# Layer 0's last two periods with output tiles between matrices, layer 1's group norm per image, first pixels loaded into room given up early

## The chip, the cores and the metric

The kernel runs on one core of one Trainium2 chip. The metric is device time in microseconds (us), the median of several runs. A core has five engines that work side by side: TensorE (PE, matrix products; its weight loads are listed apart as PEld), VectorE (DVE), ScalarE (ACT), GpSimd (POOL) and SyncE (SP), which here only issues DMA transfers. Tiles live in SBUF, products land in PSUM.

## The reference

Two images x of 512 channels and 64 x 64 pixels pass two layers, each of the form x = x + f(gn(x)); gn is a group norm of 32 groups without weights.

Layer 0's f is a deformable convolution:

```
xproj  = gn(x) @ in_w + in_b
x1     = gelu(layernorm(depthwise3x3(gn(x)) + dw_b))
offset = x1 @ off_w + off_b
mask   = softmax over 9 points of (x1 @ mask_w + mask_b), in 16 groups
out    = sum over 9 points of mask * bilinear sample of xproj at (grid + offset)
result = out @ out_w + out_b
```

Layer 1's f is attention over the 4096 pixels of an image, then a batch norm and a relu:

```
q, k = tanh(px @ Wq.T), tanh(px @ Wk.T)          # 64 wide
v    = px @ Wv.T
attn = softmax(einsum(q, k, align_w))
c    = (px + attn @ v) @ Wfc.T + bfc
f    = relu(gamma * (c - mean) * rsqrt(var + eps) + beta)
```

The change leaves the computation as it is.

## The kernel before, in words

**Layer 0** handles an image in 8 chunks of 512 pixels (8 rows), 16 chunks for both images. The stages of one chunk are Python generators, which give their instructions step by step:

- `project(i)`: the group-normed rows `xn`, and their products with `in_w` (PSUM `pq`), stored to DRAM as `xt_d`.
- `features(i)`: depthwise convolution on DVE from `xn`, layer norm, gelu.
- `weights(i)`, 27 steps: four products `po` with their additions to `o` (steps 1 to 8), the softmax's exponential (9), `tx` (10), an overflow sum called far here (11), the softmax's sums (12), `my` (13), nine steps that build the 5 x 5 weight windows `aw` out of `pk` (14 to 22), the copy `at` on ACT (23), and four transposes `p_tr` with copies to `awT` (24 to 27).
- `sample(i)`, 24 steps: eight small products `pb`, each copied into the matrix `bt` (1 to 8; all copies on ACT, but for the last chunk every second on DVE); eight products `pa` of `bt` with a fetched patch, each with four copies to `dT` (9 to 16); and the four **output tiles** `py`, the products with `out_w`, each followed by an addition to the residual `res`, its statistics into `stats2`, and the store to `x1_d` (17 to 24). The fetch of the next chunk's patches and the reads of `res` are issued inside these steps, on SP.

In layer 0's main loop the order is written out by hand (`tc.manual_schedule()`). `period(...)` takes steps of `sample(i)` (m), `weights(i + 1)` (w), `features(i + 2)` and `(i + 3)`, `project(i + 3)`, the last four transposes of `weights(i)` (v) and the output tiles of `sample(i - 1)` (y). From i = 13 on there is nothing left to project, and in i = 14 and 15 there are no features left: the period's calls for them give nothing, but the order of the rest stays. In period 14, m is chunk 14, w chunk 15, y chunk 13; in period 15 m is chunk 15, w is empty and y chunk 14. The output tiles of chunk 15 come after the loop, in `y.rest()`. Every engine is given its instructions in the order written.

**Between the layers.** Layer 0's pools are closed and layer 1's opened in the same memory. By default the first use of a pool's room waits for all tiles of closed pools that the pool lies over; with `reuse_waits="tile"` a tile waits only for those that it lies over itself. Layer 1's pixel pool `w1c` has 8 places of 8 KB, at the lowest addresses after the constants, where layer 0 keeps `xn`, `bt`, `awT` and small weights. The code then issues, on SP: the loads of `wkq` (the key and query weights side by side, in both orders) and `al`; the first two chunks of pixels (L1140); `wc`, the joined value and output weights (L1158); the next two chunks. DVE gathers both images' statistics (L1182), and `group_norm` with PE, DVE and ACT turns them into scale and shift (L602 to L620). Then ACT normalizes the first two chunks (L1173), DVE forms their sums and differences (L1151 to L1154) and those of `wc` (`wcs`, L1165 to L1168); these serve a seven-product scheme for 2 x 2 block matrices.

**Layer 1** per image: four turns of key and query products `pk` (L1305) and four `values` calls each, of seven products `pv` (L1251) in PSUM banks A0 to A5 with sums on DVE; then eight query blocks of scores (`pS`, L1211), exponentials and products `acc` (L1364) and `p` (L1402); last the batch norm over both images.

Of the kernel before, what the change touches and what calls it, by code (L numbers as in the profile page):

```python
# [9 lines left out]
F32 = mybir.dt.float32  # L10
# [7 lines left out]
P = 128  # L18
NB = 2
C = 512  # L20
KB = C // P
# [10 lines left out]
NCH = S // CH  # L32
# [5 lines left out]
DQ = 64  # L38
# [486 lines left out]
NSEQ = NB * NCH  # L525
# [45 lines left out]
def window_path(ctx: ExitStack, tc: tile.TileContext, t_in: dict, out: bass.AP, far: bass.AP, sums: bass.AP):  # L571
    nc = tc.nc
# [23 lines left out]
    nc.vector.memset(eps, EPS)  # L596
    stats2 = [const.tile([P, KB, NCH, 6], F32, name=f"stats2_{n}") for n in range(NB)]

    def group_norm_steps(mv, k, small, psum, result):
# [30 lines left out]
    with ExitStack() as l0:  # L630
# [8 lines left out]
        xt_d = [dram.tile([WIN, WIN, C], F32, name=f"xt_{n}") for n in range(NB)]  # L639
        xn = wp.tile([P, KB, ROWS + 2, W], F32, name="xn")  # L640
        bt = wp.tile([P, G, 2 * PX, PR * PC], F32, name="bt")

# [10 lines left out]
        in_w = load_w("L0_conv_in_w", C, wp)  # L653
        in_b = load("L0_conv_in_b", [P, KB], t_in["L0_conv_in_b"].rearrange("(kb p) -> p kb", p=P), wp)
# [343 lines left out]
        def period(y, v, m, w, f, g, p, more):  # L998
# [52 lines left out]
            w()  # L1051

        def value_weights():

# [46 lines left out]
    with ExitStack() as l1, tc.manual_schedule():  # L1101
        cp = l1.enter_context(tc.tile_pool(name="w1c", bufs=NCH))
        bnp = l1.enter_context(tc.tile_pool(name="w1bnp", bufs=1))
# [6 lines left out]
        with ExitStack() as at, ExitStack() as inner:  # L1110
            aw = at.enter_context(tc.tile_pool(name="w1w", bufs=1))
            wk = at.enter_context(tc.tile_pool(name="w1work", bufs=2))
            iw = inner.enter_context(tc.tile_pool(name="w1in", bufs=1, side="right"))
            vw = inner.enter_context(tc.tile_pool(name="w1v", bufs=3, side="right"))
# [6 lines left out]
            class Bank:  # L1121


                def tile(self, shape, dtype, tag, name):
                    return ps.tile(shape, dtype, tag="A1", name=name)
# [12 lines left out]
            def chunk(n, ch):  # L1138
                t = cp.tile([P, KB, CH], F32, tag="c", name="xt")
                (nc.scalar if n else nc.sync).dma_start(t, x1_d[n][ch])  # L1140
# [35 lines left out]

            pixels = {0: load_pixels(0, 0)}
# [110 lines left out]
            for n in range(NB):  # L1288
# [9 lines left out]
                for i in range(NCH // 2):  # L1298
# [4 lines left out]
                    for h in range(2):  # L1303
                        for kb in range(KB):
                            nc.tensor.matmul(  # L1305
                                pk[:, h, :], wkq[:, h, kb].rearrange("p h d -> p (h d)"), pixels[i][0][h][:, kb, :],
                                start=(kb == 0), stop=(kb == KB - 1),
                            )
# [224 lines left out]
```

## Time and profile before

| what | us |
|---|---|
| median of 3 runs | 3701.71 (3700.44 to 3704.26) |
| the profiled execution | 3707.44 |
| its span | 3705.6 |
| PE busy | 3417.9 (92%) |
| DVE busy | 2345.8 (63%) |
| ACT busy | 1304.1 (35%) |
| start of period 14's first output product (`py` L969) | 1150.55 |
| end of layer 0's last `py` | 1276.0 |
| first `pv` of layer 1 | 1293.31 |

Times in the trace count from the span's start. A line of the page's part 2 shows the span in 40 slices of 92.6 us. In a timeline a row is one run of like instructions: start, length, engine, line, what is written and read, how many; in brackets how long the engine was idle before and what released it. In a table of stretches a row gives the busy time of each engine, the granted TensorE clock (1.00 is full speed), and the share of the DMA engines. One `pb` or `pa` or `py` shows as several instructions: 16 in a row are a pair of `pb`, 16 are one `pa`, 8 are one `py` or one `po`.

### The profile page before, as it was taken

The numbers are of one execution on the slowest core, as the hardware profiler recorded it, in microseconds if no ns is written. First come the engines' busy times: TensorE is split into PE (matmuls) and PEld (weight loads), VectorE is DVE, ScalarE is ACT, GpSimd is POOL, SyncE is SP. The second block draws the span as 40 slices with busy tenths as digits, with TensorE's granted clock in tenths as the row PEclk, the third lists the DMA queues.
The fourth block names the chain that finished last, engine by engine and source line by source line (L and its number), as shares of the span: only waits on it lengthen the run. The fifth ranks groups of instructions, "written<-read, shape, count | busy, mean of one in ns | idle before, by whom it ended". The sixth has DMA issues, their size and how long they took to land.

```text
span 3705.6 us, 39010 instructions
## 1 busy us (share of the span) xinstructions
PE 3417.9 (92%) x15151; PEld 2433.8 (66%) x15151; DVE 2345.8 (63%) x3575; ACT 1304.1 (35%) x1691; POOL 291.0 (8%) x190
## 2 busy tenths in 40 slices
PE   4689998999998799999999999999999999999990
PEld 1355555555555477777777777777777777777770
DVE  5798989999996475545554554567455455545544
ACT  2476777787886321111111111221111111111114
POOL 2112111212111030000000000022000000000000
PEclk9789999999999899999999999999999999999995
DMA  7233442342432444334334333444433333243349
GB/s 240 63 98 114 135 137 83 115 133 83 127 109 78 142 157 171 126 129 139 123 108 163 122 125 130 140 155 169 149 121 111 122 138 111 101 149 121 111 162 389
DMA packets 180181, 500.06 MB, mean 135 GB/s; under 512 B 22640, under 2 KB 64368, under 8 KB 170512
## 3 DMA queue, kind: packets, MB, share of 16 engines
q1 hardware_dynamic: 176496, 473.34, 37.5%
q10 hardware_dynamic: 3456, 24.12, 1.7%
q8 instruction: 121, 1.98, 0.2%
q14 instruction: 76, 0.62, 0.0%
q0 software_dynamic: 32, 0.00, 0.0%
HBM read 406.09 MB, written 91.29 MB: 134 GB/s over the span
## 4 chain that ended last, share of the span: by engine, by line
PE 75%; DVE 15%; DMA 4%; ACT 2%; SPq 1%; issue 1%; POOL 1%; ACTq 0%; DVEq 0%; POOLq 0%
PE acc L1364 41%; DVE conv L788 8%; PE pS L1211 7%; PE p L1402 7%; PE py L969 5%; PE pq L758 4%; PE pa L949 4%; PE pv L1251 3%; PE pk L1305 1%; PE p_mean L801 1%; DVE pk L885 1%; DVE aw L890 1%; DMA patch<-xt 1%; DMA out<-ct 1%; DVE o L847 1%
## 5 line engine op out<-in xcount | busy, mean ns | idle before, releaser
L1364 PE MATMUL acc<-e,v 128*128 128x256 f32 x3072 | 768.2, 386 | 0.0
L1215 ACT ACTIVATE e<-pS 128x1024 f32<-128x1024 f32 x256 | 262.0, 1024 | 1386.4 <-PE pS L1211 1313.0
L1364 PE MATMUL acc<-tt,v 128*128 128x256 f32 x3072 | 748.2, 380 | 0.5 <-DMA v<-wv 0.5
L1364 PEld LDWEIGHTS acc<-e,v 128*128 128x128 f32 x3072 | 566.5, 190 | 233.2 <-issue 165.3
L1364 PEld LDWEIGHTS acc<-tt,v 128*128 128x128 f32 x3072 | 582.4, 190 | 91.2 <-issue 10.6
L1218 DVE TENSOR_TENSOR t<-e 128x256 f32<-128x256 f32 x256 | 108.8, 425 | 761.1 <-ACT e L1215 761.1
L788 DVE SCALAR_TENSOR_TENSOR conv<-xn,L_conv_dw_w_sb,conv 128x504 f32<-128x504 f32 (+1 forms) x512 | 399.7, 795 | 48.5 <-ACT conv L783 36.5
L1228 DVE TENSOR_TENSOR tot<-tot,e 128x512 f32<-128x512 f32 x480 | 330.1, 688 | 8.3
L949 PEld LDWEIGHTS pa<-bt,patch 96*128 96x128 f32 x2048 | 251.8, 197 | 63.1 <-issue 39.4
L1211 PE MATMUL pS<-q,kq 64*128 64x512 f32 x1024 | 289.0, 641 | 0.0
L949 PE MATMUL pa<-bt,patch 96*128 96x128 f32 x2048 | 255.3, 281 | 9.3 <-ACT dT L960 5.8
L935 ACT COPY bt<-pb 96x1024 f32<-96x1024 f32 x124 | 234.2, 2001 | 58.9 <-PE pb L930 58.9
L758 PE MATMUL pq<-L_conv_in_w_sb,xn 128*128 128x512 f32 x512 | 236.3, 605 | 4.3 <-ACT xn L748 4.3
L969 PE MATMUL py<-dT,L_conv_out_w_sb 128*128 128x512 f32 x512 | 238.0, 610 | 0.0
L1402 PE MATMUL p<-t,v 128*128 128x256 f32 x1024 | 231.4, 382 | 1.7 <-DMA v<-wv 1.7
L1402 PEld LDWEIGHTS p<-t,v 128*128 128x128 f32 x1024 | 192.1, 190 | 48.5 <-issue 21.2
L960 ACT COPY dT<-pa 32x256 f32<-32x256 f32 x496 | 179.5, 362 | 89.8 <-PE pa L949 80.9
L842 PE MATMUL po<-om_w_pg,feat 128*128 128x432 f32 x512 | 203.4, 542 | 0.0
L969 PEld LDWEIGHTS py<-dT,L_conv_out_w_sb 128*128 128x128 f32 x512 | 99.3, 197 | 119.6 <-issue 115.5
L758 PEld LDWEIGHTS pq<-L_conv_in_w_sb,xn 128*128 128x128 f32 x512 | 94.1, 194 | 109.5 <-issue 93.0
L842 PEld LDWEIGHTS po<-om_w_pg,feat 128*128 128x128 f32 x512 | 93.0, 191 | 90.5 <-issue 89.4
L1211 PEld LDWEIGHTS pS<-q,kq 64*128 64x128 f32 x1024 | 77.1, 184 | 84.9 <-issue 84.9
(203 smaller groups left out, 3731.2 us busy)
## 6 DMA issues: line engine op xcount, KB each, us to landing
v<-wv SPq DMA_DIRECT2D x252, 768.0 KB
patch<-xt SPq DMA_DIRECT2D x256, 192.0 KB
v<-wv SPq DMA_DIRECT2D x256, 128.0 KB
wv<-v SPq DMA_DIRECT2D x32, 896.0 KB
xt<-xj SPq DMA_DIRECT2D x128, 128.0 KB
res<-in_x SPq DMA_DIRECT2D x64, 256.0 KB
wx<-res SPq DMA_DIRECT2D x64, 256.0 KB
xq<-wx SPq DMA_DIRECT2D x16, 1024.0 KB
```

The lines of the kernel that those rows point to most:

```text
L758: nc.tensor.matmul(pq, xn[:, kb, 1 + 2 * t : 3 + 2 * t, :].rearrange("p r c -> p (r c)"), in_w[:, kb, :], start=(kb == 0), stop=(kb == KB ...
L788: nc.vector.scalar_tensor_tensor(dst, src, wt, dst, ALU.mult, ALU.add)
L842: nc.tensor.matmul(po[:, : 3 * GP], f[:, kb, t * P : (t + 1) * P], om_w[:, kb].rearrange("p a k g -> p (a k g)"), start=(kb == 0), stop=(k ...
L935: copy(bt[:SN].rearrange("s g q d -> s d (g q)")[:, d0 : d0 + 4, :], pb[:SN])
L949: nc.tensor.matmul(pa[:, p], xp[:SN, p, cb * P : (cb + 1) * P], bt[:SN, 4 * cb : 4 * cb + 4, PX * s + p, :], start=True, stop=True,)
L960: copy(dst, src)
L969: nc.tensor.matmul(py, out_w[:, kb, cb * P : (cb + 1) * P], dT[:, kb, :], start=(kb == 0), stop=(kb == KB - 1))
L1211: nc.tensor.matmul(pS[:, h, :], kq[r, 2 * (kp // 4) + h, c0 : c0 + P], qs[qb][r, :], start=True, stop=True)
L1215: nc.scalar.activation(e.rearrange("p a q -> p (a q)"), pS.rearrange("p h q -> p (h q)"), AF.Exp)
L1228: nc.vector.tensor_add(tots[qb], tots[qb], e2[:, h, :])
L1364: nc.tensor.matmul(acc[j][:, cb * HQ : (cb + 1) * HQ], v[:, j, cb * P : (cb + 1) * P], ops[j], start=(kp + cb == 0), stop=(kp + cb == NPAI ...
L1402: nc.tensor.matmul(p7[:, cb * HQ : (cb + 1) * HQ], v7[:, cb * P : (cb + 1) * P], t3, start=(k + cb == 0), stop=(k + cb == NPAIR + 2),)
```

## The change

Four parts, in the order in which they run:

- `wkq` and `al` move from layer 1's pool `w1in` to the constants. `wkq` holds three matrices (key, query, key) instead of four, and a slice of two of them gives either order. They are loaded by SP ahead of layer 0's main loop, in five transfers instead of six.
- `in_w` gets its room right after `xn`, ahead of `bt`; its load stays where it was.
- Periods 14 and 15 get functions of their own. `next_to_last` takes chunk 15's eight `po` steps ahead of chunk 14's transposes, and chunk 13's output tiles between the pairs of `pb`. `last_period` takes chunk 14's output tiles between the pairs of chunk 15's `pb`, and between these steps those of a group norm of image 0, whose statistics are complete after period 8.
- At the border, `w1c` and `w1in` take `reuse_waits="tile"`; the first two chunks of pixels are loaded from ACT's queue instead of SP's; image 0's norm is there already, and image 1's is spread over four places of image 0's `values` calls, with a product in bank A5.

```diff
+    norm0 = []
+    wkq = const.tile([P, KB, 3, DQ], F32, name="wkq")
+    al = const.tile([P, 1], F32, name="al2")
...
         xn = wp.tile([P, KB, ROWS + 2, W], F32, name="xn")
+        in_w = wp.tile([P, KB, C], F32, name="in_w")
         bt = wp.tile([P, G, 2 * PX, PR * PC], F32, name="bt")
...
+        def next_to_last(y, v, m, w):
+            y()
+            w(8)
+            v(4)
+            for steps, tiles in ((1, 2), (1, 2), (2, 2), (1, 1)):
+                m(2)
+                w(steps)
+                y(tiles)
+            for _ in range(4):
+                m(2)
+                w(2)
+            w(2)
+
+        def image_norm(n):
+            mv = const.tile([P, KB, 2], F32, name=f"mv2_{n}")
+            for k in range(KB):
+                nc.vector.bn_aggr(mv[:, k, :], stats2[n][:, k, :, :].rearrange("p a b -> p (a b)"))
+            yield
+            yield from group_norm_steps(mv, KB, const, ps, norm0)
+
+        def last_period(y, v, m, _):
+            norm = image_norm(0)
+            y()
+            v(4)
+            for steps in (2, 2, 2, 1):
+                m(2)
+                y(steps)
+                next(norm, None)
+            for _ in range(8):
+                m()
+                next(norm, None)
+            for _ in norm:
+                pass
...
         fetch(0, 1)
+        for k, name in enumerate(("wkT", "wqT", "wkT")):
+            nc.sync.dma_start(wkq[:, :, k, :], t_in[name].rearrange("(kb p) m -> p kb m", p=P))
+        for h in range(2):
+            nc.sync.dma_start(al[h * DQ : (h + 1) * DQ, :], t_in["L1_conv_align_w"])
...
+                if i + 2 >= NSEQ:
+                    (next_to_last if i + 1 < NSEQ else last_period)(y, v, m, w)
+                    y, v = m, w
+                    continue
                 period(y, v, m, w, f, g, Chain(project, i + 3), lambda: next(later, None))
...
-        cp = l1.enter_context(tc.tile_pool(name="w1c", bufs=NCH))
+        cp = l1.enter_context(tc.tile_pool(name="w1c", bufs=NCH, reuse_waits="tile"))
...
-            iw = inner.enter_context(tc.tile_pool(name="w1in", bufs=1, side="right"))
+            iw = inner.enter_context(tc.tile_pool(name="w1in", bufs=1, side="right", reuse_waits="tile"))
...
-            wkq = iw.tile([P, 2, KB, 2, DQ], F32, name="wkq")
-            al = iw.tile([P, 1], F32, name="al2")
-            for h in range(2):
-                nc.sync.dma_start(wkq[:, h, :, h, :], t_in["wkT"].rearrange("(kb p) m -> p kb m", p=P))
-                nc.sync.dma_start(wkq[:, h, :, 1 - h, :], t_in["wqT"].rearrange("(kb p) m -> p kb m", p=P))
-                nc.sync.dma_start(al[h * DQ : (h + 1) * DQ, :], t_in["L1_conv_align_w"])
...
-                pair = [chunk(n, 2 * i + h) for h in range(2)]
+                pair = [chunk(n, 2 * i + h, nc.scalar if n or i == 0 else nc.sync) for h in range(2)]
...
-            mv = bnp.tile([P, NB * KB, 2], F32, name="mv2")
-            for k in range(NB * KB):
-                nc.vector.bn_aggr(mv[:, k, :], stats2[k // KB][:, k % KB, :, :].rearrange("p a b -> p (a b)"))
-            both = group_norm(mv, NB * KB, bnp, Bank())
-            norms = [[t[:, n * KB : (n + 1) * KB] for t in both] for n in range(NB)]
+            def second_norm():
+                mv = bnp.tile([P, KB, 2], F32, name="mv2")
+                for k in range(KB):
+                    nc.vector.bn_aggr(mv[:, k, :], stats2[1][:, k, :, :].rearrange("p a b -> p (a b)"))
+                yield
+                yield from group_norm_steps(mv, KB, bnp, Bank(), norms[1])
+            norms = [norm0, []]
+            later = second_norm()
...
                         values(n, i, t)
+                        for _ in range({5: 1, 7: 2, 11: 2, 12: 1}.get(4 * i + t, 0) if n == 0 else 0):
+                            next(later, None)
```

More of the change, by code (lines that the diff above doesn't have):

```diff
@@ L652, in window_path @@
                 eng.dma_start(img[kb][:, h * (S // 2) : (h + 1) * (S // 2)], x_v[0, :, kb, h * (S // 2) : (h + 1) * (S // 2)])
-        in_w = load_w("L0_conv_in_w", C, wp)
+        nc.sync.dma_start(in_w, t_in["L0_conv_in_w"].rearrange("(kb p) m -> p kb m", p=P))
         in_b = load("L0_conv_in_b", [P, KB], t_in["L0_conv_in_b"].rearrange("(kb p) -> p kb", p=P), wp)
@@ L1124, in tile, with chunk @@
                 def tile(self, shape, dtype, tag, name):
-                    return ps.tile(shape, dtype, tag="A1", name=name)
-            wkq = iw.tile([P, 2, KB, 2, DQ], F32, name="wkq")
-            al = iw.tile([P, 1], F32, name="al2")
-            for h in range(2):
-                nc.sync.dma_start(wkq[:, h, :, h, :], t_in["wkT"].rearrange("(kb p) m -> p kb m", p=P))
-                nc.sync.dma_start(wkq[:, h, :, 1 - h, :], t_in["wqT"].rearrange("(kb p) m -> p kb m", p=P))
-                nc.sync.dma_start(al[h * DQ : (h + 1) * DQ, :], t_in["L1_conv_align_w"])
+                    return ps.tile(shape, dtype, tag="A5", name=name)
+            pixels = {}
             ones = iw.tile([P, P], F32, name="ones_k")
             nc.vector.memset(ones, 1.0)
-            def chunk(n, ch):
+            def chunk(n, ch, queue):
                 t = cp.tile([P, KB, CH], F32, tag="c", name="xt")
-                (nc.scalar if n else nc.sync).dma_start(t, x1_d[n][ch])
+                queue.dma_start(t, x1_d[n][ch])
                 return t
             def load_pixels(n, i):
-                pair = [chunk(n, 2 * i + h) for h in range(2)]
+                pair = [chunk(n, 2 * i + h, nc.scalar if n or i == 0 else nc.sync) for h in range(2)]
                 return pair, [cp.tile([P, 2, 2, CH], F32, tag="c", name=name) for name in ("xsa", "xsb")]
@@ L1175, in normalize @@
                     )
-            pixels = {0: load_pixels(0, 0)}
+            pixels[0] = load_pixels(0, 0)
             wc = value_output()
             pixels[1] = load_pixels(0, 1)
-            mv = bnp.tile([P, NB * KB, 2], F32, name="mv2")
-            for k in range(NB * KB):
-                nc.vector.bn_aggr(mv[:, k, :], stats2[k // KB][:, k % KB, :, :].rearrange("p a b -> p (a b)"))
-            both = group_norm(mv, NB * KB, bnp, Bank())
-            norms = [[t[:, n * KB : (n + 1) * KB] for t in both] for n in range(NB)]
+            def second_norm():
[6 more added lines that the diff above has]
+            later = second_norm()
             w7 = aw.tile([P, 2, 7, HC], F32, name="w7")
@@ L1305, in window_path @@
                             nc.tensor.matmul(
-                                pk[:, h, :], wkq[:, h, kb].rearrange("p h d -> p (h d)"), pixels[i][0][h][:, kb, :],
+                                pk[:, h, :], wkq[:, kb, h : h + 2].rearrange("p h d -> p (h d)"), pixels[i][0][h][:, kb, :],
                                 start=(kb == 0), stop=(kb == KB - 1),
```

## The prediction

> **What bounds the kernel now.** I read the page's slices first. TensorE is busy nearly throughout, but for the prologue, the end, and a dip where layer 0 gives way to layer 1 (slices 13 and 14, 1111 to 1297 us); the same slices granted less clock.
>
> ```profile
> PE   4689998999998799999999999999999999999990
> PEclk9789999999999899999999999999999999999995
> ```
>
> The table of stretches then shows what the dip is made of:
>
> ```profile
> 1140.00:1150.00 10.00, 4.20 (x25) 4.01 (x24) 9.65 (x13) 8.30 (x11) 0.00 (x0) 0.73 0.57 184
> ...
> 1154.60:1165.00 10.40, 7.40 (x37) 4.58 (x37) 1.45 (x2) 7.34 (x7) 1.43 (x1) 0.68 0.38 140
> 1165.00:1180.00 15.00, 14.93 (x77) 7.41 (x75) 1.85 (x4) 11.38 (x7) 0.00 (x0) 1.00 0.00 1
> 1213.00:1240.00 27.00, 17.80 (x107) 13.82 (x108) 8.46 (x7) 11.31 (x11) 0.00 (x0) 0.50 0.24 72
> ...
> 240.00:250.00 10.00, 8.07 (x46) 4.54 (x45) 8.30 (x13) 8.03 (x9) 1.44 (x1) 1.00 0.73 236
> 1276.00:1293.30 17.30, 9.31 (x20) 4.39 (x21) 8.02 (x20) 7.33 (x10) 0.00 (x0) 0.80 0.91 334
> ```
>
> The first number after the length is PE's busy time, the eighth column the clock. From 1213 to 1240 no engine is busy for more than two thirds: PE waits, and what it does runs at half clock. TensorE's timeline gives the waits and two prices of each product:
>
> ```profile
> 1096.42 1.14 PE L930 MATMUL pb<-awT,sel 25*96 25x256 f32 x16 [0.83 <-ACT awT L902]
> ...
> 1150.55 4.07 PE L969 MATMUL py<-dT,L_conv_out_w_sb 128*128 128x512 f32 x8
> 1156.94 2.42 PE L901 MATMUL p_tr<-ident,at 128*128 128x128 f32 x16 [2.33 <-ACT at L893]
> ...
> 1213.85 3.67 PE L901 MATMUL p_tr<-ident,at 128*128 128x128 f32 x16 [4.92 <-ACT at L893]
> 1218.20 2.05 PE L930 MATMUL pb<-awT,sel 25*96 25x256 f32 x16 [0.68 <-ACT awT L902]
> 1222.18 2.12 PE L930 MATMUL pb<-awT,sel 25*96 25x256 f32 x16 [1.93 <-ACT bt L935]
> ...
> 1234.29 6.64 PE L949 MATMUL pa<-bt,patch 96*128 96x128 f32 x32 [2.01 <-ACT bt L935]
> ```
>
> A pair of `pb` costs 1.06 to 1.14 at full clock, 2.05 here; two `pa` 6.64 against 3.58. At the border:
>
> ```profile
> 1284.74 8.73 PE L1305 MATMUL pk<-xt,wkq 128*128 128x512 f32 x16 [3.78 <-ACT xt L1173]
> 1293.31 1.89 PE L1251 MATMUL pv<-wc,xt 128*128 128x256 f32 x8
> 1295.74 1.99 PE L1251 MATMUL pv<-wcs,xsa 128*128 128x256 f32 x8 [0.55 <-DVE wcs L1166]
> ```
>
> Layer 0's last `py` ends at 1276.0; `pk` starts 8.7 us later, at part clock. Here SP's queue decides: the pixel loads stand behind the last stores of `res` (issued from 1277.24, first used at 1283.83, 6.6 us for two), while the group norm runs beside them and ends at 1283.3. Behind 1316 PE never stands still for long, and layer 1's code per block is untouched: what counts is when the `pv` begin.
>
> [...] 1.00 drops to 0.50 behind the idle 1140.8 to 1147 and 1208.8 to 1213.8, stays there at some 50% busy, and returns after about 5 us of solid work; the stretch from 240 shows 1.00 kept at 81% busy. [...]
>
> **The change, part by part.** Every duration is the trace's, full clock unless said.
>
> *Period 14, from 1150.55.* The period's start doesn't move, since period 13 is untouched. Chunk 13's first `py` ends at 1154.6; the clock is back at about 1152. Now four `po` follow at once, 4 x 3.10 = 12.4, to 1167.0 (their gelu ended at 1149.5), where PE waited 2.33 and then ran cold. Chunk 14's transposes (1.97) and the last `awT` copy (0.8) come behind them, to 1169.8: 9.9 later than before. From there ACT sets the pace: eight `bt` copies of 1.86 (14.9), the exponential with its table load (1.96), the far sum (1.35), the first pair 1.1 and handshakes 0.8 give 1189.9, against 1180.5. PE has in this stage 4 x 1.06 + 3 x 3.44 = 14.6, so three `py` are hidden that before stood between the `pa`. Eight `pa` of 1.79 then end at 1204.4 (before: 1205.3). DVE: its last addition ends near 1186, then 0.77 + 8 x 1.57 = 13.3 of windows to 1199.3, hidden. ACT's `at` copy stands behind the last `dT` copies (1206.0) and takes 2.92: 1208.9, against 1213.8. Of 12.4 moved into idle time, 4.9 remain. PE's first `py` of chunk 14 fits ahead of it.
>
> *Period 15.* Transposes and copies: first `pb` at 1212.5 (before 1218.2, cold). Three rounds of a pair and a `py`, 4.5 each, plus 0.36 for the norm's first product: 1226.4; the copies, 1.86 on ACT and DVE side by side, hide under the `py`. Fourth pair and its copies, 1.06 + 2.1: 1229.5. Eight `pa` 14.3; the norm's root on ACT puts 1.6 (table load 1.28, 0.3) between their copies, and these alternate between ACT and DVE, so add 1.6 and 1.4: 1246.8. Four `py` 13.75, with up to 1.6 for the last `dT` copies: 1262.0 against 1276.0. **Gain so far 14.0**; of it 8.5 is clock (transposes 1.7, four pairs 4 x 1.0, `pa` 3.0), which I take as given because no gap on this path exceeds 2 us.
>
> The norm's aggregation and small DVE steps (1.0, 0.9) and second product (0.39) lie under `py`, `bt` copies and the wait for the last `bt`; uncovered they would add 2.3. SP: fetching chunk 15's patches (5.6 us per half) starts when a patch is free, about 1197 and 1204, and is needed at 1229 and 1239; the `res` reads move with their steps and keep some 8 us. What is late next is ACT's `bt` copies in period 14.
>
> *Border.* Places 0 and 1 of the pixel pool (16 KB) lie within `xn` and `in_w` (18 KB), read last at about 1118 (convolution) and 1092 (`pq`). ACT is through with its `dT` copies at 1248.4, issues two loads, which land 6.6 later at 1255, and normalizes eight times 0.72 to 1261: all under the last `py`. Nothing else waits on ACT there. The PSUM pool keeps its default wait, so `pk` needs the last addition of `res` (0.2 + 0.75): 1263.0, then 16 x 0.43 = 6.9 to 1269.9. SP's next issue is `wc`; before it went out 4.27 after the last `py`, held by the landing of `res`, so now at 1266.3, and takes 5.2 (the second image's: 2439.96 to 2445.16): 1271.5. There the `pv` begin, with 1.6 idle. DVE's four sums (4.7) are over by 1268.5; two `wcs` (1.4) by 1272.9, and the third product comes at 1273.2, before 1295.74. **Gain 22.5.**
>
> *Given back.* Image 1's norm inside the `values` calls: two small products 0.75 on PE, two table loads (2.6) on ACT, whose calls leave it some 3 of 6 us idle; 1.0. ACT meets `wfcT` earlier: the loads behind `wc` are 4 MB at about 400 GB/s (the border's DMA rate), landing near 1278.5, up to 5 us after ACT wants them; six PSUM banks take most, 1.0. The early loads of `wkq`: some 3 us of SP issue ahead of period 0, where SP already stands idle (109 to 114) or waits 26 us for a place; bounds -1 to +3, I take 0.5.
>
> Sum: 22.5 - 1.0 - 1.0 - 0.5 = 20.0. Span 3705.6 - 20.0 = 3685.6; the profiled execution reports 3707.44 and the median is 3701.71, so I set **3681.7** against the median.
>
> **Rivals.**
> *The early room is not there (transfer as late as before).* If the pixel tiles still wait for the end of layer 0, or the ACT queue reaches them late, they land 6.8 after the last `py`, the sums follow the normalizing, and the third product is again 19.7 behind it: 8.5 lost, 3690.2. For it: the loads were issued only at 1277.24. Against: they stood behind stores on SP, and the overlapped tiles are long dead.
> *ScalarE becomes the bound.* Period 14 is paced by ACT with 18.2 us of copies and sums; if handshakes or `pa` behind it cost as much as the reorder saves, in both periods, the 14.0 goes and the border's 8.5 less 2.5 stays: 3695.7. For it: 9.9 us of delay to `awT`. Against: period 15 shares its copies with DVE.
> *TensorE stays at half clock (slower).* In the new periods PE works about 91 us at full clock from 1154.6 to the end (`po` 12.4, transposes 4, `pb` 8.5, 7 + 4 `py` 38, `pa` 28.6). The ACT-paced stage leaves it 75 to 80% busy. Each us of that work done at half rate costs one more; from 20 us of it on the gain is gone, from 27.4 it is slower by over 0.2%; with a third of it, 30 us, 3711.7. For it: before, 17.8 busy us of 27 stayed at 0.50. Against: 81% kept 1.00.
>
> **How the numbers follow.** The likeliest course 0.68, its own range 3677 to 3687 (clock and handshakes +-3, `wc` +-2). Late pixels 0.14 at 3690. ScalarE 0.09 at 3696, which is within 0.2% (7.4 us, about what a measurement of this kernel can tell from no change: 3694.3 to 3709.1). Half clock 0.07 at 3712. A smaller rest (0.02) lies lower. Faster 0.84, same 0.09, slower 0.07. The range takes in the first two: 3674 to 3693.
>
> **What would show it.** In the profile after: four `po` in a row behind the `py` at 1150.6; `bt` copies on ACT without a break to about 1190; clock 1.00 from 1155 to the border; `py` between the pairs of `pb`; last `py` ending near 1262; two loads on ACT's queue near 1248, `pk` about 1 us behind the last `py`, `pv` 8 to 10 behind it. Wrong if the pixel loads are issued after the last `py`, if `at` of chunk 15 ends after 1212, if the clock reads 0.50 in period 15, or if `pv` in image 0 stand waiting for banks by more than 3 us.

## The result, and the profile after

The changed kernel takes **3686.89 us** (median of 5 runs, 3683.94 to 3688.61) against 3701.71 before: 14.8 us less, a ratio of 0.9958 with a 95% interval of 0.9947 to 0.9969. In a second series it was 3689.50 against 3703.27, 0.9961 [0.9947, 0.9975]. The two profiled executions lie further apart, 3685.08 against 3707.44 (spans 3683.3 and 3705.6); the experiments say why, as far as it is known.

The slices of the page of the kernel after, TensorE's busy share and its clock:

```profile
PE   4589998999998999999999999999999999999990
PEclk9789999999999999999999999999999999999995
```

The dip at slices 13 and 14 is gone from both lines. TensorE's timeline of the kernel after, from period 14 to the first values products (start, length, what, and in brackets the idle time before it):

```profile
1149.52 4.06 PE L976 MATMUL py<-dT,L_conv_out_w_sb 128*128 128x512 f32 x8
1153.42 11.76 PE L849 MATMUL po<-om_w_pg,feat 128*128 128x432 f32 x32
1165.02 1.96 PE L908 MATMUL p_tr<-ident,at 128*128 128x128 f32 x16
...
1187.88 17.99 PE L956 MATMUL pa<-bt,patch 96*128 96x128 f32 x128 [3.78 <-ACT bt L942]
1205.70 3.60 PE L976 MATMUL py<-dT,L_conv_out_w_sb 128*128 128x512 f32 x8
1210.37 1.99 PE L908 MATMUL p_tr<-ident,at 128*128 128x128 f32 x16 [1.07 <-ACT at L900]
...
1230.58 17.07 PE L956 MATMUL pa<-bt,patch 96*128 96x128 f32 x128 [1.76 <-ACT bt L942]
...
1262.28 7.10 PE L1356 MATMUL pk<-xt,wkq 128*128 128x512 f32 x16 [0.89 <-issue]
1270.09 1.97 PE L1302 MATMUL pv<-wc,xt 128*128 128x256 f32 x8 [0.70 <-DMA wc<-wvfc]
...
1294.42 1.13 PE L1302 MATMUL pv<-wc,xsb 128*128 128x256 f32 x4 [2.51 <-DVE v L1306]
```

The four `po` stand in a row, and chunk 15's transposes wait 1.07 us instead of 4.92. The last `py` ends at 1261.4, 111.9 us behind the period's start (before: 125.4). At the border `pk` follows 0.9 us behind the last `py` (before: 8.7) and the third values product 10.5 us behind it (before: 19.8). The row of 128 `pa` in period 14 took 17.99, where the forecast had 14.3, and stands behind a gap of 3.78. The table of stretches of the same kernel (length, busy time of PE, of its weight loads, DVE, ACT, POOL, then the clock):

```profile
1184.00:1188.00 4.00, 0.22 (x5) 0.13 (x2) 3.90 (x6) 3.71 (x2) 0.00 (x0) 1.00 0.17 66
1188.00:1192.00 4.00, 4.00 (x19) 4.00 (x20) 3.83 (x6) 0.37 (x2) 0.00 (x0) 0.50 0.00 0
1192.00:1196.00 4.00, 4.00 (x26) 4.00 (x25) 3.83 (x6) 2.05 (x6) 0.00 (x0) 0.65 0.00 0
...
1226.40:1230.60 4.20, 2.44 (x22) 1.19 (x20) 3.07 (x7) 1.86 (x1) 0.00 (x0) 1.00 0.17 64
1230.60:1234.00 3.40, 3.40 (x24) 3.40 (x24) 1.58 (x4) 0.76 (x3) 0.00 (x0) 0.76 0.60 144
1234.00:1238.00 4.00, 3.93 (x27) 3.77 (x27) 1.63 (x6) 2.43 (x5) 0.00 (x0) 0.78 0.60 205
...
1230.58:1247.50 16.92, 16.72 (x129) 16.24 (x130) 7.60 (x19) 6.66 (x16) 0.00 (x0) 0.90 0.27 78
```

Behind the gap the mean clock was 0.50 for 4 us and 0.65 for the next 4; behind the shorter gap of period 15 it was 0.76 and 0.78. The last row is the whole row of period 15's `pa`. ScalarE's timeline of the kernel after:

```profile
1207.41 2.90 ACT L900 COPY at<-aw 128x1600 f32<-128x1600 f32 x1
...
1248.54 0.83 ACTq L1185 DMA_DIRECT2D xt<-wx  x2
1253.36 5.83 ACT L1218 ACTIVATE xt<-xt,gn_bi,gn_sc 128x512 f32<-128x512 f32 x8 [4.46 <-DMA xt<-wx]
...
1277.93 0.62 ACT L1321 COPY w<-v 128x512 f32<-128x512 f32 x1 [5.47 <-DMA v<-in_wfcT]
```

The pixels are requested at 1248.5, under chunk 15's products, and normalized by 1259.2, before the last `py` ends. The `at` copy follows the row before it with no idle time. ACT then waits 5.47 us for the `wfcT` weights, and PE stands 2.51 us before its products at 1294.42, in the fourth values call.

### The profile page after: what moved, and what is told of

It reads as the page before. It is cut to its first block, busy times and chain, and to the rows that moved or that the text cites. A ratio compares the mean times of both kernels' runs of the same rounds, so it can differ in the third digit from the quotient of the medians.

```text
span 3683.3 us, 39025 instructions
## 1 busy us (share of the span) xinstructions
PE 3410.6 (93%) x15155; PEld 2430.9 (66%) x15155; DVE 2344.1 (64%) x3581; ACT 1307.4 (35%) x1694; POOL 291.5 (8%) x190
## 4 chain that ended last, share of the span: by engine, by line
PE 76%; DVE 14%; DMA 4%; ACT 2%; SPq 1%; issue 1%; POOL 1%; ACTq 0%; DVEq 0%; POOLq 0%
PE acc L1417 42%; DVE conv L795 8%; PE pS L1262 7%; PE p L1455 7%; PE py L976 5%; PE pa L956 4%; PE pv L1302 4%; PE pq L765 4%; PE pk L1356 1%; PE p_mean L808 1%; DMA patch<-xt 1%; DMA out<-ct 1%; DVE o L854 1%; DMA in_w<-in_L_conv_in_w 1%; DVE rstd L827 1%
## 5 line engine op out<-in xcount | busy, mean ns | idle before, releaser
L765 PE MATMUL pq<-in_w,xn 128*128 128x512 f32 x512 | 235.8, 604 | 4.1 <-ACT xn L755 4.1
L765 PEld LDWEIGHTS pq<-in_w,xn 128*128 128x128 f32 x512 | 93.9, 194 | 108.8 <-issue 93.2
```

Of the source, the lines that this page charges most:

```text
L765: nc.tensor.matmul(pq, xn[:, kb, 1 + 2 * t : 3 + 2 * t, :].rearrange("p r c -> p (r c)"), in_w[:, kb, :], start=(kb == 0), stop=(kb == KB ...
```

## The experiments

The traces are compared by landmarks, in us: **at** is from period 14's first `py` to the end of chunk 15's `at` copy, **p15** from there to the end of layer 0's last `py`, **third** from there to the third values product, **rest** from there to the end of the span. `at` + p15 + third is called the stretch.

| kernel | at | p15 | third | stretch | rest | time, ratio |
|---|---|---|---|---|---|---|
| before, first profile | 63.3 | 62.2 | 19.8 | 145.2 | 2409.9 | 3701.71 |
| e1_before_again | 60.6 | 60.9 | 19.6 | 141.1 | 2409.9 | 3703.09, 1.0001 |
| after, first profile | 60.8 | 51.1 | 10.5 | 122.4 | 2411.4 | 3686.89, 0.9958 |
| e4_after_again | 60.3 | 51.2 | 10.4 | 121.9 | 2413.2 | 3689.50, 0.9961 |
| e2_periods_only | 60.9 | 50.9 | 20.2 | 132.1 | 2409.5 | 3693.08, 0.9972 |
| e3_border_only | 60.6 | 63.8 | 10.5 | 135.0 | 2411.2 | 3698.55, 0.9987 |
| e5_pool_waits | 61.0 | 51.7 | 19.2 | 131.9 | 2409.8 | 3695.56, one run |
| e6_sp_queue | 60.3 | 51.2 | 18.7 | 130.2 | 2409.6 | 3692.86, one run |
| e7_norm_late | 61.1 | 51.0 | 20.0 | 132.0 | 2409.4 | 3693.83, one run |
| e8_fill | 60.6 | 60.6 | 19.6 | 140.8 | 2409.8 | 3705.01, one run |
| e9_last_only | 60.6 | 51.7 | 10.7 | 122.9 | 2412.9 | 3688.63, 0.9960 |
| e10_p14_mixed | 54.4 | 51.1 | 10.4 | 115.9 | 2411.4 | 3680.72, 0.9937 |
| e11_border_early | 61.0 | 51.7 | 12.9 | 125.6 | 2409.4 | 3687.18, 0.9956 |
| e12_both | 55.6 | 50.5 | 12.9 | 119.0 | 2409.3 | 3679.43, 0.9936 |

**Does the first profile of before stand for the kernel? And which half brings what?** e1 is the kernel before and e4 the kernel after, unchanged.

> The kernel before, unchanged, with a second profiled execution. The profiled executions of the two kernels lie 22.4 us apart, their medians 14.8. Theory A (the change saves some 22, and single executions wander by some us in parts the change doesn't touch): ratio 1.000, the second profile's time from period 14's first output product (1150.55 in the first) to the third group of value products (1295.74) is again 145.2 within 1 us, and what differs lies outside. Theory B (the half clock in periods 14 and 15 comes and goes from execution to execution): the same stretch is 3 to 8 us shorter than 145.2, and the span nearer to 3700.

> The changed kernel again, in one session with the two halves. Theory A: ratio 0.994 to 0.9965, that is the sum of the two halves within 3 us. If the halves help each other (a warm clock at the border), it is more than the sum; if they share a gain, less.

e2 has only the two new periods (and the old border, with no norm steps in between); e3 has only the border, the early norm put into the old period 15:

```diff
 # e2, against before
+                if i + 2 >= NSEQ:
+                    (next_to_last if i + 1 < NSEQ else last_period)(y, v, m, w)
+                    y, v = m, w
+                    continue
 # e3, against after: every period in the old order
-                if i + 2 >= NSEQ:
-                    (next_to_last if i + 1 < NSEQ else last_period)(y, v, m, w)
-                    y, v = m, w
-                    continue
+                if i + 1 == NSEQ:
+                    later = image_norm(0)
```

> The kernel before with the two new functions for periods 14 and 15 alone, without the norm's steps; the border stays as it was. The profiles put the end of layer 0's last output product 14.8 us earlier after the change, 1.0 of it from before period 14, and the norm's root put 1.9 into the row of samples. Theory A: 14 to 16 us faster, 3687. Theory B: 6 to 10 us faster, 3694. Rival (the border takes the gain back, since pixels and norm wait for other things): under 5 us faster.

> The changed kernel with the old order in periods 14 and 15 (image 0's norm in the gaps of period 15's spreading products). The profiles put the third group of value products 10.7 us behind the last output product, before 19.7: 9.0 saved, and about 1.5 given back later. Theory A: 7 to 8 us faster, 3694. If the early loads of the key and query weights cost in the prologue: 3 to 5 us faster. If pixels arrive late under the old order: no change.

e1 measured 3703.09 (ratio 1.0001 [0.9993, 1.0009]), but its profiled execution has a stretch of 141.1 where the first profile has 145.2. TensorE's timeline of e1, at period 14 and at period 15:

```profile
1146.95 5.27 PE L969 MATMUL py<-dT,L_conv_out_w_sb 128*128 128x512 f32 x8
1153.36 1.97 PE L901 MATMUL p_tr<-ident,at 128*128 128x128 f32 x16 [1.14 <-ACT at L893]
1156.16 1.14 PE L930 MATMUL pb<-awT,sel 25*96 25x256 f32 x16 [0.83 <-ACT awT L902]
...
1222.86 2.21 PE L930 MATMUL pb<-awT,sel 25*96 25x256 f32 x16 [1.78 <-ACT bt L935]
1227.08 6.26 PE L949 MATMUL pa<-bt,patch 96*128 96x128 f32 x32 [2.01 <-ACT bt L935]
```

This is theory B of e1 (3 to 8 us shorter). Here period 14 begins at full clock (`p_tr` 1.97 and `pb` 1.14, against 2.42 and 2.05 in the first profile); period 15 is for the most part at half clock in both. Of the 4.1 us, 2.7 lie in period 14 and 1.3 in period 15. The first profile is the odd one: in the four other traces with the old order in period 14 (e1, e3, e8, e9) `at` is 60.6 each time, chunk 13's first `py` takes 5.08 to 5.27 and the wait behind it 1.14 to 1.31. In the first profile the clock came back earlier (1.00 from 1152.0 to 1154.6), so this `py` took only 4.07; the wait behind it grew to 2.33, and the clock was lost again (0.50 from 1160 to 1165). In the kernel after and in e10 a `py` of 4.06 and 4.05 did no such harm: `po` follow at once.

So some 4 us of the 22.3 between the first profiles belong to one execution of before, and what comes ahead of period 14 differs too: period 14 starts between 1145.6 and 1154.2 in the fourteen traces, in no order with the edits. Against e1 the change is worth 141.1 - 122.2 = 18.9 in the stretch (122.2 is the mean of the two profiles of after), less 1.5 to 3.3 given back in the rest: 15.6 to 17.4, where the medians say 14.8 and 13.8. The 1 to 3 us between them are not explained. The two executions of the kernel after differ in the clock, too. TensorE's timeline of e4, the `pa` of period 14:

```profile
1193.65 16.36 PE L956 MATMUL pa<-bt,patch 96*128 96x128 f32 x128 [3.78 <-ACT bt L942]
```

Behind the same gap of 3.78 the row takes 16.36, in the first profile of after 17.99.

The halves: e2 is 10.2 us below before (0.9972 [0.9962, 0.9983]), e3 4.7 (0.9987 [0.9981, 0.9994]). They add up to 14.9, and the whole is 13.8 in the same series, so neither hides the other. e2 stays below its theory A (14 to 16) and at the edge of B (6 to 10): A was read from the first profile. e3 measured what was expected if the early loads of `wkq` cost time, but its landmarks put the loss elsewhere. Its `third` is shorter by 9.1, yet it gains only half of that: its `p15` is 2.9 longer, because in the old order the norm's two products wait 3.00 and 2.43 us for DVE with the `pb` pairs behind them, and the rest is 1.3 longer. 19.6 - 10.5 - 2.9 - 1.3 = 4.9, with 4.7 measured. TensorE's timeline of e3:

```profile
1214.73 0.57 PE L607 MATMUL gn_p<-mv,gmat_sb 128*128 128x8 f32 x2 [3.00 <-DVE mv L1078]
1215.23 2.05 PE L937 MATMUL pb<-awT,sel 25*96 25x256 f32 x16
1219.71 0.59 PE L616 MATMUL gn_p<-gn_d,gmat_sb 128*128 128x4 f32 x2 [2.43 <-DVE gn_d L613]
```

**Which of the border's three parts is needed?** Each run takes one part out of the kernel after.

```diff
 # e5
-        cp = l1.enter_context(tc.tile_pool(name="w1c", bufs=NCH, reuse_waits="tile"))
+        cp = l1.enter_context(tc.tile_pool(name="w1c", bufs=NCH))
 # e6
-                pair = [chunk(n, 2 * i + h, nc.scalar if n or i == 0 else nc.sync) for h in range(2)]
+                pair = [chunk(n, 2 * i + h, nc.scalar if n else nc.sync) for h in range(2)]
 # e7: both images' norm at the border, as before
-            norm = image_norm(0)
+            norm = iter(())
...
+            both = group_norm(mv, NB * KB, bnp, Bank())
...
+            later = iter(())
```

> The changed kernel, but the pixel pool w1c waits for all of layer 0's tiles under it again. It is read from the last output product's end to the third group of value products: 10.7 us in the changed kernel, 19.7 before. If the early room is what lets the pixels come early: loads issued on ACT only about 1 us behind the last output product, landing 6 to 7 later, 18 to 20. If ACT's queue alone would do: 10.7, as in the changed kernel.

> The changed kernel, but the first two chunks of pixels are loaded from SP's queue. If they stand behind the last stores of res: 17 to 19 us from the last output product's end to the third group of value products. Rival: SP is given them ahead of those stores (the loads of the key and query weights were issued at 1217.7 before, though written behind layer 0's end): 10 to 11 us, and the stores wait for nothing.

> The changed kernel, but both images' norm is computed at the border in one piece, as before; pixels come early. The norm ended 7.3 us behind the last output product before. If norm and pixels were two waits side by side, taking away one alone gives nothing: key products 8 to 9 us behind the last output product and the third group of value products 18 to 20. If the pixels alone had set the time: 11 to 13.

All three have `third` back at 18.7 to 20.0, near the 19.6 to 20.2 of the old border; the five traces that have all three parts and nothing else changed at the border (after, e3, e4, e9, e10) have 10.4 to 10.7, so one trace each can show it. `pk` starts 7.4, 7.7 and 8.4 us behind the last `py`. Each part taken out costs `third` 8 to 9.6 us, though the other two are there; the rest is 1.6 to 3.8 shorter then, where ACT waits 0.4 us at most for `wfcT`. ScalarE's timeline of e5, the load of the pixels:

```profile
1265.55 0.83 ACTq L1185 DMA_DIRECT2D xt<-wx  x2
```

SP's timeline of e6, the same load:

```profile
1263.97 0.87 SPq L1185 DMA_DIRECT2D xt<-wx  x2
```

ScalarE's timeline of e7:

```profile
1249.73 0.82 ACTq L1185 DMA_DIRECT2D xt<-wx  x2
...
1268.04 1.28 ACT L620 ACT_TABLE_LOAD   x1 [17.95 <-DVE gn_var L619]
...
1270.10 5.74 ACT L1218 ACTIVATE xt<-xt,gn_bi,gn_sc 128x512 f32<-128x512 f32 x8 [0.47 <-DVE gn_bi L625]
```

In e5 the early place on the queue is no use, since the room isn't free for it; in e6 the room is free, but the load stands behind the last stores; in e7 the pixels are there early and wait for their scale and shift. The three conditions stand side by side, and the latest decides.

**Is it the clock that period 15 gains?** The forecast put 8.5 of its 14.0 us in layer 0 down to full clock. e8 is the kernel before with its old order, plus four rounds of four products of `out_w` with itself in period 15, read by nobody, where PE had been idle: work added, none left out.

```diff
+        def fill():
+            t = ps.tile([P, C], F32, tag="mm", name="p_fill")
+            for _ in range(4):
+                nc.tensor.matmul(t, out_w[:, 0, 0:P], out_w[:, 0, :], start=True, stop=True)
...
             y()
+            if last:
+                fill()
             v(4)
...
                 m(2)
+                if last and len(fills) < 3:
+                    fills.append(fill())
```

> The kernel before with four fillers in period 15 (each four products of out_w with itself, 3.44 us at full clock, read by nobody): one behind chunk 14's first output product, one behind each of the first three pairs of spreading products. TensorE does 13.8 us more and nothing else moves. If the half clock costs what was forecast there (transposes 1.7, samples 3.0, pairs 4 x 1.0 of which the fillers' own length takes back most): transposes at 2.0 instead of 3.7, pairs at 1.1, the first two samples at 3.6 instead of 6.6, and from the first pair to the first sample about 17 us instead of 16.1; in sum the last output product ends 3 to 5 us earlier, counted from period 15's at copy. If the clock were no cause: later by 1 us or more.

TensorE's timeline of e8:

```profile
1213.29 1.97 PE L901 MATMUL p_tr<-ident,at 128*128 128x128 f32 x16 [1.50 <-ACT at L893]
1216.09 1.14 PE L930 MATMUL pb<-awT,sel 25*96 25x256 f32 x16 [0.83 <-ACT awT L902]
1217.15 3.70 PE L1002 MATMUL p_fill<-L_conv_out_w_sb 128*128 128x512 f32 x8
...
1233.38 5.44 PE L949 MATMUL pa<-bt,patch 96*128 96x128 f32 x32 [2.08 <-ACT bt L935]
```

For transposes and pairs the filler does what it was to do: `p_tr` costs 1.97 instead of 3.67, each pair 1.14, where in e1 three of four take 2.1 to 2.2. The first two `pa`, behind a gap of 2.08, still take 5.44 (expected 3.6). `p15` falls only from 60.9 or 62.2 to 60.6; the 3 to 5 us expected aren't there. The tables of stretches show why, from the transposes' start to the first `pa`, in e1, in e8 and in the kernel after:

```profile
1207.59:1227.08 19.49, 11.33 (x80) 8.17 (x81) 7.61 (x5) 9.79 (x8) 0.00 (x0) 0.59 0.32 94
1213.29:1233.38 20.09, 17.18 (x104) 8.70 (x105) 7.78 (x5) 9.68 (x8) 0.00 (x0) 1.00 0.30 90
1210.37:1230.58 20.21, 17.65 (x108) 9.37 (x109) 13.01 (x19) 9.68 (x8) 0.00 (x0) 1.00 0.38 140
```

The stage lasts 19.5 us at a mean clock of 0.59, and 20.1 and 20.2 at full clock (20.4 in the first profile of before, at 0.50). In e8 three fillers take 11.10 of PE's 17.18 us; in the kernel after three `py` take 11.10 of 17.65, and the norm's two products 0.67. What remains, transposes and pairs, costs 6.1 and 5.9 us against 11.3 in e1, and PE's idle time is 2.9 and 2.6 against 8.2. So 11 us of products found room in a stage of nearly the same length: half of the room came from the waits (5.3 and 5.6), half from the clock (5.3 and 5.5).

e8 spends this room on work that nobody needs, and gains 0.2 us in `p15` against e1 (1.6 against the first profile); its one time, 3705.01 beside 3701.96 for the kernel before in the same series, shows no gain either. The kernel after puts three `py` there, which no longer stand behind: from the first `pa` to the last `py`'s end it needs 30.8 us, e1 41.3 and e8 40.5. That is the gain of period 15, some 10 us of work moved into room that waits and clock make in equal parts. The clock alone, bought with filler, brings nothing. e8 can't say what full clock would bring with empty rounds; that stays open.

**Where did period 14's gain go?** `at` is 60.8 after, 63.3 in the first profile of before, but 60.6 in e1. e9 takes `next_to_last` out; e10 leaves it in with another order: one `po` ahead of the transposes, so that `awT` isn't late, and one behind each of the first three pairs; of chunk 13's `py` two between the pairs and the `pa`, one between the `pa`:

```diff
 # e9
-                if i + 2 >= NSEQ:
-                    (next_to_last if i + 1 < NSEQ else last_period)(y, v, m, w)
+                if i + 1 >= NSEQ:
+                    last_period(y, v, m, w)
 # e10, next_to_last
             y()
-            w(8)
+            w(2)
             v(4)
-            for steps, tiles in ((1, 2), (1, 2), (2, 2), (1, 1)):
-                m(2)
-                w(steps)
-                y(tiles)
-            for _ in range(4):
+            for tiles in (0, 0, 2):
                 m(2)
                 w(2)
-            w(2)
+                y(tiles)
+            w()
+            m(2)
+            y(2)
+            w()
+            m(2)
+            w(2)
+            m(2)
+            w()
+            y(2)
+            w(2)
+            m(2)
+            w(2)
+            y()
+            m(2)
+            w(6)
```

> The changed kernel with the old order in period 14 (period 15 and the border as changed). From period 14's first output product to its end of the at copy: 60.8 us in the changed kernel, 63.3 in the first profile of before, 60.6 in the second. Theory (the new order of period 14 wins only what the half clock cost in that one execution): 60.6 within 1, and a time within 0.1% of the changed kernel's, ratio to before 0.9955 to 0.997. Theory of the forecast (4.9 us from period 14): 63 to 66, and a ratio of 0.9965 to 0.9985.

> The changed kernel with a third order in period 14: one product po ahead of the transposes, the other three between the pairs of spreading products, two output tiles behind the third and fourth pair, one between the samples. If ScalarE's copies, started 9.3 us late behind four po, are what eats period 14's gain: awT is ready 10 instead of 20 us after the period's first product, the at copy ends at 53 to 56 instead of 60.8, and the kernel is 4 to 8 us faster than the changed one, 3680 to 3684, ratio 0.9935 to 0.9955. If DVE's chain of windows sets the time: 58 to 61 and no change.

e9 measures 3688.63 (0.9960 [0.9946, 0.9974]), the time of the kernel after. `at` is 60.6 in the four traces with the old order at full clock and 60.3 to 61.1 in the seven with `next_to_last`: as written it brings nothing, but for an execution like the first of before. The `at` copy of chunk 15 in ScalarE's timeline of e9, the old order:

```profile
1207.93 2.89 ACT L900 COPY at<-aw 128x1600 f32<-128x1600 f32 x1 [3.87 <-DVE aw L897]
```

and of e10:

```profile
1204.51 2.90 ACT L900 COPY at<-aw 128x1600 f32<-128x1600 f32 x1 [0.70 <-DVE aw L897]
```

and VectorE's last window sum in the kernel after:

```profile
1197.02 0.76 DVE L897 TENSOR_TENSOR aw<-aw,pk 128x576 f32<-128x576 f32 x1
```

In the old order ACT stands idle 3.87 us for the last window sum on DVE, until 57.7 us behind the period's start. In the kernel after DVE's last `aw` ends at 1197.8, 48.3 behind the start, so the early `po` do what they are for; but the copy starts at 1207.41, 57.9 behind it, with no idle time, directly behind ACT's `dT` copies. One wait was taken away, and another of the same height stood behind it: `po` ahead of the transposes put the `bt` copies' start at 1168.9, 19.4 behind the period's start (e9: 10.4, e10: 10.7), PE then idles 3.78 us for the last of them, and the first `pa` behind run at half clock (0.50 from 1188 to 1192). In e10 neither happens. TensorE's timeline of e10:

```profile
1159.76 1.96 PE L908 MATMUL p_tr<-ident,at 128*128 128x128 f32 x16
...
1184.19 7.47 PE L956 MATMUL pa<-bt,patch 96*128 96x128 f32 x64 [0.26 <-ACT bt L942]
1191.49 3.60 PE L976 MATMUL py<-dT,L_conv_out_w_sb 128*128 128x512 f32 x8
1194.92 7.36 PE L956 MATMUL pa<-bt,patch 96*128 96x128 f32 x64
...
1207.46 1.99 PE L908 MATMUL p_tr<-ident,at 128*128 128x128 f32 x16 [1.74 <-ACT at L900]
```

The gap before the first `pa` is 0.26, the 128 `pa` cost 14.8 instead of 18.0, and `at` is 54.4, 6.4 less than after, of which 3.2 are the `pa`. DVE sets the copy again, 51.5 behind the start. How much of the rest is the earlier `bt` copies and how much the place of the `py` isn't separated. e10 takes **3680.72**, 0.9937 [0.9923, 0.9951]: 7.9 less than e9 on the same chip. It is faster than both kernels: its slowest of five runs, 3682.18, lies below the fastest of ten of the kernel after, 3683.94.

**Can the give-back be had as well?** e11 is the kernel after with `wc` and the `wfcT` weights requested from ACT's queue right behind the first pixels, and with per-tile waits for six more pools (weights, work tiles, values and PSUM); e12 has this and e10's order.

```diff
+            wk = at.enter_context(tc.tile_pool(name="w1work", bufs=2, reuse_waits="tile"))
...
-                nc.sync.dma_start(t, wc_d)
+                queue.dma_start(t, wc_d)
...
+            wc = value_output(nc.scalar)
+            wfs = []
+            for j in range(2):
+                wfs.append(vv.tile([P, 7, HC], F32, name="v")[:, :4, :].rearrange("p (r i) c -> p r i c", r=2))
+                nc.scalar.dma_start(
+                    wfs[j].rearrange("p r i c -> p r (i c)"),
+                    t_in["wfcT"].rearrange("(j r p) m -> j p r m", p=P, r=2)[j],
+                )
```

> The changed kernel with more loaded early: wc and the two halves of wfcT from ACT's queue behind the first pixels, and tile-wise waits for the pools of weights, work tiles, values and PSUM. If the 2.5 us that TensorE stands before the fourth values call (1294.42) come from wfcT landing late, they vanish; key products start up to 0.9 earlier, value products 0.7; from the last output product's end to the third group of value products 9 instead of 10.5, and behind it 2410 instead of 2411.4 to 2413.2: 3 to 5 us faster than the changed kernel. If DVE's slow sums beside GpSimd alone make that stand: 1 to 2 us.

> The changed kernel with the third order in period 14 and the early loads of the run before. If both hold, the sum: 8 to 12 us faster than the changed kernel, 3676 to 3680, ratio 0.9925 to 0.9945.

The slow sums are there in the kernel after: three of DVE's sums of the second values call (L1314 to L1316, from 1286.60 on) take 2.46 to 2.57 us each, while GpSimd forms the next pixels' sums (1286.19 to 1296.26); the same lines take 0.42 in the first call and in the two behind it. The sums from 1293.96 on, beside GpSimd's last, take 0.41 to 0.42.

e11 wins the rest back (2409.4, as before; PE's wait in the fourth values call is 0.30 instead of 2.51) and loses it again at the border (`third` 12.9, expected 9): 3687.18, no change, where 3 to 5 us were expected. ScalarE's timeline of e11:

```profile
1247.33 0.82 ACTq L1185 DMA_DIRECT2D xt<-wx  x2
1248.40 0.33 ACTq L1203 DMA_DIRECT2D wc<-wvfc  x1
1260.21 0.92 ACTq L1227 DMA_DIRECT2D v<-in_wfcT  x2
1261.18 5.74 ACT L1218 ACTIVATE xt<-xt,gn_bi,gn_sc 128x512 f32<-128x512 f32 x8 [13.49 <-DVE res L981]
```

The two requests of `wfcT` stand on ACT until layer 0's last `py` is through (1260.2 to 1261.1; what ACT waited for is named as DVE's last addition to `res`), and the pixels are normalized behind them, 13.9 us behind their request (1247.33 to 1261.18) instead of 4.8 in the kernel after (1248.54 to 1253.36). That it is the room of `wfcT` that wasn't free is argued from the order of the rows; no run moved it. The trace shows the price: from 1248.7 to 1260.2, 11.5 us, ACT does nothing, though by the kernel after's 4.8 its pixels would have been there at about 1252 (an estimate). Issuing `wfcT` behind the normalizing might keep both gains; that wasn't tried. e12 takes 3679.43 (0.9936 [0.9922, 0.9950]), 7.8 below e11, as e10 is 7.9 below e9; from e10 it can't be told apart, so what it gains is e10's order alone.

## Why the prediction was right, and where its steps were wrong

The time came out 5.2 us above the predicted 3681.7, inside the range and inside the likeliest case's own. Against its own anchor, the first profile of before, the sum of 20.0 stands beside 22.3; against the medians it stands beside 14.8. Of its three gains the border's came for the reasons given and period 15's in part; period 14's 4.9, against e1, didn't come at all, and that is about what the total is short of. By steps, forecast gain beside the gain against the first profile and against e1:

| step | forecast | first profile | e1 |
|---|---|---|---|
| period 14, to the end of `at` | 4.9 | 2.5 | -0.2 |
| period 15, to the last `py` | 9.1 | 11.1 | 9.8 |
| border, to the third product | 8.5 | 9.3 | 9.1 |
| given back | -2.5 | -1.5 to -3.3 | -1.5 to -3.3 |

- **The anchor.** The sum was made against one execution and moved whole onto the median. 4.1 us of it were that execution's own by e1: 2.7 in period 14, which lost the clock at its start as in none of the four other traces with the old order, and 1.3 in period 15. The prediction saw 5.7 us between the execution and the median and didn't ask whether the stretch it meant to shorten had them. This is the largest error of the sum.
- **"Of it 8.5 is clock ... which I take as given."** For transposes and pairs the sizes were right: 5.7 forecast, and 5.5 against e1 or 6.2 against the first profile measured (11.33 or 12.09 to 5.88). For the `pa`, 3.0 forecast, it failed: their PE time is 16.87 after, 17.71 in e1 and 18.08 in the first profile, so 0.8 to 1.2. The three terms as listed add up to 8.7, and the idle stretch read as beginning at 1140.8 begins at 1141.2 (5.80 before 1146.97). As a gain of its own the clock isn't shown: e8 has it and wins nothing, since what it saves only counts where useful work fills it.
- **Period 15.** Here the total was saved by luck in part. The forecast took 3.0 off the row of `pa` for the clock and added 3.0 for copies and the norm's root; measured, PE works 16.72 of its 16.92 us at a clock of 0.90, so little of either came, and they cancel. The wait of up to 1.6 for the last `dT` copies didn't come either (the last four `py` follow at once and take 13.90), which makes most of the 2.0 by which the period beat its forecast against the first profile.
- **"No gap on this path exceeds 2 us."** If the path includes period 14, it was wrong: 3.78 there, 3.7 us of dear `pa` behind it. The forecast's own figures, 14.6 us of PE's work in a stage of 20.1, left 5.5 idle. Nor was 2 us, the author's estimate, a safe bound: a gap of 1.76, in a stretch (1226.4 to 1230.6) with PE busy for 2.44 of 4.2, was followed by a clock of 0.76. And the same gap of 3.78 cost the `pa` less in e4, 16.36 instead of 17.99, so in these two executions a gap's length alone didn't decide.
- **Period 14's 4.9.** The order of events was as written (`bt` copies without a long break to 1187.8, `at` behind the last `dT` copies at 1210.3, forecast 1208.9, from a start 1.0 earlier). Two terms failed. The new value came out 2.4 too long, 60.8 instead of 58.4, mainly because the `pa` took 3.7 more; and the value before, 63.3, is 60.6 in e1. The rival in which ScalarE becomes the bound holds in this period alone, and e10 takes the gain that it had eaten.
- **The border.** These landmarks were within 1.4 us: pixel requests 1248.54 (1248.4), `pk` 0.9 behind (1.0), first `pv` 1270.09 (1271.5), with `wc` ending last (0.70 idle, forecast 1.6). The rival with late pixels is what e5 and e6 look like, with `third` at 19.2 and 18.7 for its 19.7. `in_w` was last read at 1089, not 1092, which changes nothing.
- **Given back.** ACT waited 5.47 for `wfcT` (up to 5), PE 2.51 (1.0). The rate of about 400 GB/s behind these terms is that of the first profile's border, 373 to 430 between 1282.0 and 1293.3. e11 ties PE's wait to `wfcT`: with the weights early it is 0.30. The loads of `wkq` ahead of layer 0, put at 0.5, show nowhere above the spread of period 14's start; SP issues them from 78.5 to 82.6, in a pause of its queue that is 14.5 us long after and 14.6 before. The norm of image 0 was costed at 2.3 if uncovered; e3's `p15`, where it was, is 1.6 to 2.9 longer than the two profiles of before.
- **Half clock.** It came back twice, for some 8 us each and in part, behind the gaps in periods 14 and 15 (0.50 and 0.65, 0.76 and 0.78); the rival needed 20 us of work at half rate to take the gain.

## What to carry to other kernels

Before a sum is anchored to a profile, look at a second execution of the same kernel in the very stretch that is to shrink. When a wait is taken away, ask at what time the next one ends: here DVE's windows came 9 us earlier and ACT's copies, as late as the windows had been, took the whole gain, which a mixed order then got back. Filling waits with products counts where the products are ones that had to be done anyway: filler kept the clock up (1.00 in e8 against 0.59 in e1) and gained nothing (0.2 us in `p15`). Several parallel conditions for one start have to be removed together, and a request that must wait for room belongs behind the work that its engine could do meanwhile (in e11 two such requests held ACT for 11.5 us).

## What the runs showed of the hardware that had not been expected

- Executions of one kernel wander with no edit: period 14's start by 3.6 us in the kernel before (1150.55 and 1146.95) and by 4.7 in the kernel after (1149.52 and 1154.18), and the stretch by 4.1 between two executions of before, with the clock in period 14 at half in one and full in the other (the first pair of `pb` 2.05 and 1.14 us).
- The gap behind which the clock falls isn't a fixed length here: 3.78 us cost the `pa` 3.7 us in one execution and 2.1 in another of the same kernel (17.99 and 16.36 against 14.3), and gaps of 1.76 and 2.08 were followed by mean clocks of 0.76 for 3.4 us (kernel after) and 0.72 for 6 (e8, 1234 to 1240).
- An earlier full clock can cost. In one execution of the kernel before, with chunk 13's first `py` at 4.07 instead of 5.27 us, the wait behind it was 2.33 instead of 1.14, and the half clock came back (0.50 from 1160 to 1165).
- Full clock bought with filler was worth nothing: the same stage took 19.5 us at a mean clock of 0.59 with empty waits and 20.1 at full clock with 11.1 us of filler in them.
